# The head of a fused Mamba and mixture-of-experts layer: first norm earlier in the order, identity products ahead of it, modulation vectors by transposes, copies spread over the batches

## The chip, the cores and the metric

One core of a Trainium2 chip runs the whole program in one launch. Five engines work side by side and wait for each other on semaphores: TensorE (PE, matmuls; PEld is its weight load), VectorE (DVE), ScalarE (ACT), GpSimdE (POOL) and SyncE (SP, which issues most of the DMAs). The metric is device time in microseconds (us) of one execution; less is better.

## The reference

x has 8 batches of 512 tokens with 256 features. From a vector c of 256 numbers per batch, six modulation vectors are made; then a gated Mamba-like block with a linear state of size 16, and a mixture of 8 experts of which each token uses one:

```python
mod = (_silu(L0_c) @ L0_wmod).reshape(L0_c.shape[0], 6, 1, -1)
sa, ca, ga, sb, cb, gb = (mod[:, 0], mod[:, 1], mod[:, 2], mod[:, 3], mod[:, 4], mod[:, 5])
ga = (2 * (ga >= 0) - 1) * jnp.maximum(jnp.abs(ga), 0.25)
gb = (2 * (gb >= 0) - 1) * jnp.maximum(jnp.abs(gb), 0.25)
h = _layernorm(x, axis=-1) * (1 + ca) + sa
x = x + ga * _L0_attn_ref(h, ...)
h = _layernorm(x, axis=-1) * (1 + cb) + sb
x = x + gb * _L0_ffn_ref(h, ...)
```

The block: a norm with gamma and beta, a projection to 1024 columns split in x_part and z, a causal convolution of four taps over x_part with silu, a recurrence `state = state @ A.T + u_t @ Bm.T`, the gate `(xc_t + state @ Cm) * sigmoid(z_t)`, a projection back to 256, and a residual. The expert part: softmax of `x @ wr + br`, the best expert of each token and the share of the best among the best two, and then `gelu(x @ w1 + b1) @ w2 + b2` of that expert, times the share. All numbers are float32.

## The kernel before

**Two parts.** The first part works through the batches one after another. Per batch, `stage_norm` loads the tokens (xt), takes statistics on DVE with one power on POOL (rs), normalizes on ACT (xn), applies the modulation (bc) on DVE to give h, normalizes again and brings the result to features by rows through PE transposes (tp_a) and ACT (xnT). `stage_base` forms the residual on POOL (in h, in place), the output weights times the gate (wb_) and transposes the residual (tp_b, baseT). `stage_conv` computes the state inputs (pv, v), scans them in three steps of products (pd), projects four chunks (px), and convolves them on DVE (sv, three taps each) with a silu on ACT. `stage_out` projects the other four chunks (px, tz), adds the state's output (pc), and multiplies back (po). `stage_place` writes the rows (xr) to a table xp_d in DRAM, copies the second half's modulation vectors of a batch beside them (1.5 MB a batch, from modb_d), and scatters token numbers sorted by expert to ids_d. After batch 5 an early table names four blocks of tokens, whose expert work can begin ahead of the rest. The second part works through blocks of up to 256 tokens of one expert: gather of rows (xg), transposes (tp), layer 1 (ph, gl), layer 2 (py), and a scatter of the result (out). After its planned list it reads the number `filled` of blocks in use on every engine and branches around two optional groups of blocks; with these inputs both are passed over.

**Set-up.** Ahead of the batches, `three` computes a batch's vectors as rows from half of the modulation weights (wm): pm and pg on PE, then seven DVE steps, among them the gate's magnitude (mag). It is called for batch 0 with 128 equal rows (bc0), and in `vectors` for all batches at once with 8 rows, for each half (mod0, mod1), which are written to mod_d and modb_d. `vectors` computes some of the same again by feature (pf, modT) for the router weights (rw, rg, rsum, wr2). `states` builds powers of the 16x16 state matrix by squaring it eight times (pa, at: each step a PE product, then a copy), and from these lt, cs (pq), more (pmo, pm28), wb (pw1), lx and lm (pm2), and from the transposed input weights (pw, wx) the state input weights bw (pb). wb is what the first scan step (pd) of every batch multiplies with.

**What sets the order.** Nothing is issued as it is written. The class `Plan` records every instruction of a part with its engine, an assumed length, what it must come after, the buffers it uses, and a due time `nc.due`; `order` then lists them: of all that could go next, the one that could start first, and among equals the one due first. Due times run backwards through the dependences. `emit` issues each engine's instructions in this order, and each engine keeps to its own list. A pool with a fixed number of buffers holds each kind of tile (ps_x has three PSUM buffers, ps_s one, ps_o and ps_t two); a tile waits until an older one is released. In the helper the recorded operations all stand on two lines (L159 for the first of a run of PE instructions and for all other engines, L154 for the following ones), so the profile's groups are told apart by tile names.

Of the kernel before, what the change touches and what calls it, by code (L numbers as in the profile page):

```python
# [18 lines left out]
P = 128  # L19
# [16 lines left out]
class Plan:  # L36
# [20 lines left out]
    def __init__(self, tc, last=None):  # L57

        self.tc, self.nc = tc, tc.nc
        self.free = {q: last.free[q] if last else 0.0 for q in self.REACH}  # L60
        self.ops, self.touched, self.tiles = [], {}, {}
        self.due, self.also, self.pairing = 0.0, ([], []), 0
        for name in self.QUEUES:
            setattr(self, name, self.Engine(self, name))
# [71 lines left out]
    def add(self, name, op, args, kw):  # L136
# [12 lines left out]
        if queue == "PE" and last and last["queue"] == "PE" and (  # L149
            last["out"] == out.tensor.name or (self.pairing and last["pairing"] == self.pairing)  # L150
        ):

            me = last
            me["calls"].append(lambda: getattr(getattr(self.nc, name), op)(*args, **kw))  # L154
            me["length"] += 0.05 if self.pairing else length
        else:
            me = dict(
                i=len(self.ops), queue=queue, due=self.due,
                calls=[lambda: getattr(getattr(self.nc, name), op)(*args, **kw)],  # L159
                before=set(), after=set(), uses=set(), length=length + (0.3 if small else 0.0),  # L160
                size=0, out=out.tensor.name, pairing=self.pairing,
            )
            self.ops.append(me)
        if op == "activation":
            me["table"] = {AF.Gelu: 1, AF.Silu: 2, AF.Tanh: 2}.get(args[2] if len(args) > 2 else None)
        if "dma" in op:
            me["size"] = 4
            for _, n in out.ap:
                me["size"] *= n
            me["indirect"] = "indirect" in op  # L170
# [20 lines left out]
    def order(self):  # L191
# [19 lines left out]
        order, table = [], 2  # L211
# [14 lines left out]
        while len(order) < len(ops):  # L226
            best = None
            for q, l in ready.items():
                for o in l:
# [6 lines left out]
                    if best is None or (at, o["due"]) < best[:2]:  # L236
                        best = (at, o["due"], o)
            assert best is not None, "no buffer for any instruction that could be next"
            at, _, o = best
            table = o.get("table") or table  # L240

# [6 lines left out]
            free[o["queue"]] = at + o["length"]  # L248
            end = at + o["length"]
# [40 lines left out]
def adaln_mamba_moe_kernel(  # L290
# [140 lines left out]
    with tc.tile_pool(name="wa", bufs=1) as wa, tc.tile_pool(  # L431
# [81 lines left out]
        def vectors():  # L513

            for half, to in ((0, mod_d), (1, modb_d)):
                mod = wa.tile([B, 3, D], FP, name=f"mod{half}", tag="mod")
                three(mod, sT, half, B)
                nc.sync.dma_start(out=to, in_=mod.rearrange("b i d -> b (i d)"))


            pf = ps_o.tile([P, 6, B], FP, name="pf", tag="po")
            for m in range(6):
                w, at_m = (wmh[1], m) if m < 4 else (wmh[0], m)
                for k in range(KD):
                    nc.tensor.matmul(
                        pf[:, m], lhsT=w[:, k, at_m * P : (at_m + 1) * P],
                        rhs=sT[:, k, :], start=(k == 0), stop=(k == KD - 1),
                    )
            nc.vector.tensor_copy(modT[:, 0:2], pf[:, 0:2])
            nc.vector.tensor_scalar(modT[:, 2:4], pf[:, 2:4], 1.0, None, ALU.add)  # L530
            gT = modT[:, 4:6]
            nc.vector.tensor_copy(gT, pf[:, 4:6])
            mT = wa.tile([P, KD, B], FP, name="mT")
            nc.vector.scalar_tensor_tensor(mT, gT, -1.0, gT, ALU.mult, ALU.max)
            nc.vector.tensor_scalar(mT, mT, 0.25, None, ALU.max)
            nc.vector.tensor_scalar(gT, gT, 0.0, 2.0, ALU.is_ge, ALU.mult)
            nc.vector.scalar_tensor_tensor(gT, gT, -1.0, mT, ALU.add, ALU.mult)
# [52 lines left out]
        def states():  # L590


            for j in range(STEPS - 1):
# [5 lines left out]
                nc.vector.tensor_copy(at[:, j + 1], pa)  # L599
# [4 lines left out]
            nc.vector.tensor_copy(a3t, pa3)  # L604
# [6 lines left out]
            for i in range(CH):  # L611
                for j in range(i + 1):
                    nc.vector.tensor_copy(lt[:, i, j * SP : j * SP + DS], power[i - j])
                nc.vector.tensor_copy(lt[:, i, DS : 2 * DS], power[i + 1])
# [13 lines left out]
            nc.vector.tensor_copy(more[:, 0:5], pmo)  # L628
            pm28 = ps_s.tile([DS, DS], FP, name="pm28", tag="ps")
            nc.tensor.matmul(pm28, lhsT=at[:, 4, 0], rhs=more[:, 0], start=True, stop=True)  # L630
            nc.vector.tensor_copy(more[:, 5], pm28)
# [3 lines left out]
            pw1 = ps_s.tile([P, SPAN[0], DS], FP, name="pw1", tag="ps")  # L635
# [4 lines left out]
            nc.vector.tensor_copy(wb[:, :, DS:], pw1)  # L640
# [4 lines left out]
            for j, m in enumerate(gaps):  # L645
                nc.vector.tensor_copy(lx[:, j, DS:], m)
            ix = wa.tile([DS, 2 * DS], FP, name="ix")
            nc.vector.memset(ix, 0.0)
            nc.vector.tensor_copy(ix[:, DS:], i16)
            pm2 = ps_s.tile([2 * DS, len(gaps), 2 * DS], FP, name="pm2", tag="ps")  # L650
# [3 lines left out]
            nc.vector.tensor_copy(lm, pm2)  # L654
# [13 lines left out]
            pb = ps_s.tile([P, KD, DS], FP, name="pb", tag="ps")  # L668
# [6 lines left out]
            nc.vector.tensor_copy(bw[:, :, 0:DS], pb)  # L675
# [223 lines left out]
        def stage_place(t):  # L899
# [12 lines left out]
            for n in range(b + 1 if b else 0, min(b + 2, B)):  # L912
                nc.sync.dma_start(
                    out=xp_d[n * L : (n + 1) * L, OWN:ROW], in_=modb_d[n].partition_broadcast(L)
                )
# [181 lines left out]
        PERIOD = 36.0  # L1097
        cs, wb, lm, bw = states()
        rw, rsum, wr2 = vectors()
        for b in range(B):  # L1100
            nc.due = (b + 3) * PERIOD
            t = stage_norm(b)
            stage_base(t)
# [285 lines left out]
```

## Time and profile before

| | us |
|---|---|
| three runs | 585.32, 589.22, 590.69 |
| median | 589.22 |
| profiled execution, its own time | 587.33 |
| span of the profiled execution | 585.2 |
| PE busy | 562.3 (96%) |
| DVE busy | 348.1 (59%) |
| ACT busy | 211.0 (36%) |
| POOL busy | 209.3 (36%) |
| first projection px of batch 0 on PE | 37.48 |
| first product pv of batch 1 on PE | 79.49 |
| end of po of batch 7 on PE | 313.8 |
| first layer 2 py of the second part | 321.8 |
| end of the last py | 579.6 |

A line of the page that begins with an engine's name gives its busy tenths in 40 equal slices of the span (14.6 us each); PEclk is the clock that PE was granted, in tenths. A line of the timeline has start, length, engine, line, operation, out<-in and the number of instructions, then in brackets the idle time before it and what ended it. A 128x512 product in float32 shows as two instructions of 0.43 us. A line of the waits names who waited for whom: us in total, times, longest. The span starts at the first instruction of any engine.

### The profile page before, as it was taken

How to read it: one execution, taken by the hardware profiler on the slowest of the kernel's cores; microseconds unless marked ns; L12 is line 12 of the kernel's file. 1: busy time of each engine (PE TensorE's matmuls, PEld its weight loads, DVE VectorE, ACT ScalarE, POOL GpSimd, SP SyncE). 2: the span in 40 equal slices, each digit the busy share in tenths (PEclk: the TensorE clock that was granted, in tenths of full speed). 3: DMA queues.
4: the chain of work that ended last, by engine and by line, in shares of the span. 5: the costliest groups of instructions: out<-in, count | busy, mean ns of one | idle time of the engine just before them, and what ended most of it. 6: DMA issues, size and time to landing. Idle time of an engine off the chain costs nothing.

```text
span 585.2 us, 8673 instructions
## 1 busy us (share of the span) xinstructions
PE 562.3 (96%) x2882; PEld 428.0 (73%) x2882; DVE 348.1 (59%) x1087; ACT 211.0 (36%) x404; POOL 209.3 (36%) x330
## 2 busy tenths in 40 slices
PE   4999999999999999999999798999999999999996
PEld 2454766757576676757578687878988988988895
DVE  4879968798987968686595924163433433522312
ACT  2328454455363445252342021222422222332140
POOL 1423673635446372621333421342242222322112
PEclk9779999999999999999999999999999999999999
DMA  7348999420210101010553969997887787886000
GB/s 277 129 129 183 271 254 258 71 91 0 64 38 1 38 2 36 1 37 1 161 175 91 239 198 398 394 396 266 282 279 275 274 251 242 276 286 194 15 18 20
DMA packets 58703, 96.73 MB, mean 165 GB/s; under 512 B 9852, under 2 KB 41854, under 8 KB 58656
## 3 DMA queue, kind: packets, MB, share of 16 engines
q1 hardware_dynamic: 50720, 72.98, 41.4%
q0 software_dynamic: 7936, 23.17, 11.1%
q8 instruction: 24, 0.39, 0.3%
q14 instruction: 23, 0.19, 0.2%
HBM read 86.42 MB, written 22.81 MB: 187 GB/s over the span
## 4 chain that ended last, share of the span: by engine, by line
PE 73%; DMA 17%; DVE 3%; issue 3%; SPq 1%; POOL 1%; ACT 0%; POOLq 0%; ACTq 0%
PE py L154 10%; PE px L159 10%; PE po L154 9%; PE px L154 9%; DMA out<-ot,ids 8%; PE ph L159 6%; PE ph L154 6%; PE pc L154 3%; PE po L159 3%; PE pd L154 3%; DMA ids<-ids_d 3%; DMA ids_d<-tok,row 2%; DMA w1t<-in_w 2%; PE py L159 2%; DMA xg<-xp_d,ids 1%
## 5 line engine op out<-in xcount | busy, mean ns | idle before, releaser
L159 ACT ACTIVATE gl<-ph,b1t 128x256 f32<-128x256 f32 (+1 forms) x152 | 68.3, 452 | 179.5 <-PE ph L154 159.9
L154 PE MATMUL py<-w2t,gl 128*128 128x256 f32 x476 | 108.3, 379 | 0.0
L154 PEld LDWEIGHTS py<-w2t,gl 128*128 128x128 f32 x476 | 90.4, 190 | 12.3
L159 PE MATMUL ph<-hT,w1t 128*128 128x256 f32 (+1 forms) x304 | 84.1, 358 | 5.4 <-DMA w1t<-in_w 3.0
L154 PE MATMUL ph<-hT,w1t 128*128 128x256 f32 (+1 forms) x304 | 83.8, 357 | 0.0
L159 POOL DMA_INDIRECT out<-ot,ids x36 | 36.4, 1012 | 130.7 <-DVE ot L159 121.0
L159 DVE TENSOR_TENSOR ot<-py,b2t 128x256 f32<-128x256 f32 x34 | 14.4, 424 | 113.0 <-PE py L154 113.0
L159 DVE SCALAR_TENSOR_TENSOR sv<-u,pt,sv 128x512 f32<-128x512 f32 x96 | 71.9, 759 | 4.3 <-ACT sv L159 4.3
L159 POOL DMA_INDIRECT xg<-xp_d,ids x36 | 38.9, 1080 | 87.3 <-DMA ids<-ids_d 48.3
L159 PE MATMUL px<-xnT,wi 128*128 128x512 f32 x128 | 69.6, 625 | 0.0
L154 PE MATMUL px<-xnT,wi 128*128 128x512 f32 x128 | 66.2, 599 | 0.0
L159 PEld LDWEIGHTS ph<-hT,w1t 128*128 128x128 f32 x304 | 54.4, 190 | 12.2 <-issue 3.6
L154 PEld LDWEIGHTS ph<-hT,w1t 128*128 128x128 f32 x304 | 55.3, 190 | 6.2
L154 PEld LDWEIGHTS px<-xnT,wi 128*128 128x128 f32 x128 | 24.6, 192 | 31.2 <-issue 31.2
L159 POOL DMA_INDIRECT ids_d<-tok,row x32 | 34.5, 1077 | 24.2 <-DVE row L159 13.2
L159 ACT COPY u<-px 128x512 f32<-128x512 f32 x32 | 18.7, 585 | 67.0 <-PE px L154 66.4
L159 ACT ACTIVATE tz<-px 128x512 f32<-128x512 f32 x32 | 19.0, 595 | 51.1 <-PE px L154 50.3
L159 POOL TENSOR_TENSOR rs<-ve,nhalf 128x4 f32<-128x4 f32 x16 | 18.8, 1174 | 44.9 <-DVE ve L159 32.2
L159 PEld LDWEIGHTS px<-xnT,wi 128*128 128x128 f32 x128 | 21.3, 192 | 17.4 <-issue 16.5
L159 DVE COPY hT<-tp 128x512 f32<-128x512 f32 (+1 forms) x20 | 12.7, 634 | 35.4 <-PE tp L154 27.4
L159 DVE TENSOR_TENSOR xr<-po,h 128x256 f32<-128x256 f32 x32 | 13.5, 423 | 30.6 <-PE po L154 30.4
L159 DVE TENSOR_TENSOR hg<-hg,xg 128x256 f32<-128x256 f32 x72 | 29.3, 421 | 1.1
(347 smaller groups left out, 949.8 us busy)
## 6 DMA issues: line engine op xcount, KB each, us to landing
w1t<-in_w SPq DMA_DIRECT2D x19, 1024.0 KB
w2t<-in_w SPq DMA_DIRECT2D x19, 1024.0 KB
xp_d<-modb_d SPq DMA_DIRECT2D x8, 1536.0 KB
xp_d<-xr SPq DMA_DIRECT2D x8, 520.0 KB
xt<-in_x SPq DMA_DIRECT2D x8, 512.0 KB
bc<-mod_d SPq DMA_DIRECT2D x7, 384.0 KB
b2t<-in_b SPq DMA_DIRECT2D x19, 128.0 KB
w<-in_w SPq DMA_DIRECT2D x2, 1024.0 KB
```

The source lines that it names most:

```text
L154: me["calls"].append(lambda: getattr(getattr(self.nc, name), op)(*args, **kw))
L159: calls=[lambda: getattr(getattr(self.nc, name), op)(*args, **kw)],
```

## The change

Four things change. (1) The norm of batch 0 is recorded ahead of `states` and `vectors`, due at 20, and the order has three new rules: until its own time 24, an engine takes the one due first among all that could start within 0.3 us of the earliest; until 100, PE takes a product with many columns where the last 3.4 us held few; and idle PE time ahead of 20 is filled with products of the identity with itself, twice side by side (pwarm). The built order holds one such run of six, ahead of all other PE work. (2) In `vectors`, the by-feature vectors modT come from transposes of the rows mod0 and mod1 (six transposes and one DVE copy in place of 24 products and seven DVE steps), and `vectors` waits for xnT of batch 0. (3) Small copies in `states` move from DVE to ACT, and pw1, pm2 and pb move from the PSUM pool ps_s to ps_x. (4) The copies of the modulation vectors from modb_d into xp_d, of which seven were issued in one run after mod1, are spread: none at batch 0, batch 0's at 1, batch 1's at 2, two each at 3, 4 and 5; each waits for xr of the batch at which it stands.

In the built order, pw, pb and two pq now stand ahead of tp_a of batch 0 on PE, and pm and pg of mod0 between tp_a and px; the other half's pm and pg, the other two pq, the transposes of the output weights (pw2) and the end of the state chain stand behind the first px. On SP, the state matrix is loaded third and not first; loads of xt and bc now stand ahead of all copies from modb_d. In the second part the order is the same but for two neighbours and the place of the read of `filled`: on PE it stood behind the last py, and now stands two products into the last group of eight.

```diff
@@ Plan.__init__, add
+        self.hold, self.thick, self.warm = 0.0, 0.0, None
...
+        if queue == "PE":
+
+            n = 1
+            for c in ins[1 if op == "matmul" else 0].shape[1:]:
+                n *= c
+            me["dense"] = me.get("dense", 0) + (2 if op == "matmul" else 1) * n * ins[0].shape[0] / P
@@ Plan.order
-        while len(order) < len(ops):
+        while len(order) < len(ops) + fillers:
...
+                if could:
+                    mine = min(could)
+                    if mine[0] < self.hold:
+
+                        mine = min((c for c in could if c[0] < mine[0] + 0.3), key=lambda c: c[1:3])
+                    if q == "PE" and mine[0] < self.thick:
+
+
+                        t, l = mine[0], mine[3]["length"]
+                        lately = sum(
+                            d * max(0.0, b - max(a, t + l - 3.4)) / (b - a) for a, b, d in streamed[-40:]
+                        )
+                        if lately + mine[3]["dense"] < 1800:
+                            dense = [c for c in could if c[3]["dense"] > 900 * c[3]["length"] and c[0] < t + 0.3]
+                            mine = min(dense, key=lambda c: c[1:3]) if dense else mine
...
+            if self.warm and o["queue"] == "PE" and at < self.warm[0]:
+
+                slow = 2 if at < self.warm[1] else 1
+                n = int(0.8 * (at - free["PE"]) / (slow * self.warm[2]))
+                if n > 0:
+                    order.append(dict(i=-1, at=free["PE"], queue="PE", calls=[self.warm[3]] * n))
...
@@ vectors
+            pf = ps_o.tile([P, 6, B], FP, name="pf", tag="po")
             for half, to in ((0, mod_d), (1, modb_d)):
+
+                nc.due = (1 + 2 * half) * PERIOD
                 mod = wa.tile([B, 3, D], FP, name=f"mod{half}", tag="mod")
                 three(mod, sT, half, B)
                 nc.sync.dma_start(out=to, in_=mod.rearrange("b i d -> b (i d)"))
...
+                for m, i in ((0, 1), (2, 0)) if half else ((4, 2),):
+                    for k in range(KD):
+                        nc.tensor.transpose(
+                            pf[:, m + k], mod[:, i, k * P : (k + 1) * P], ident[0:B, 0:B]
+                        )
+            nc.due = 3 * PERIOD
+            nc.vector.tensor_copy(modT, pf)
@@ states (likewise a3t, lt, more, wb, lx, ix, lm, bw; pw1, pm2 and pb from ps_s to ps_x)
-                nc.vector.tensor_copy(at[:, j + 1], pa)
+                nc.scalar.copy(at[:, j + 1], pa)
@@ stage_place
-            for n in range(b + 1 if b else 0, min(b + 2, B)):
-                nc.sync.dma_start(
-                    out=xp_d[n * L : (n + 1) * L, OWN:ROW], in_=modb_d[n].partition_broadcast(L)
-                )
+
+            for n in ((), (0,), (1,), (2, 3), (4, 5), (6, 7), (), ())[b]:
+                with nc.wanting(done=[xr]):
+                    nc.sync.dma_start(
+                        out=xp_d[n * L : (n + 1) * L, OWN:ROW], in_=modb_d[n].partition_broadcast(L)
+                    )
@@ the body
         PERIOD = 36.0
+
+        pwarm = ps_o.tile([P, 2, P], FP, name="pwarm", tag="po")
+        twice = ident.unsqueeze(1).to_broadcast([P, 2, P])
+        plan.hold, plan.thick = 24.0, 100.0
+        plan.warm = (20.0, 7.8, 0.47, lambda: chip.tensor.matmul(
+            pwarm, lhsT=ident, rhs=twice, start=True, stop=True
+        ))
+        nc.due = 20.0
+        t = stage_norm(0)
+        nc.due = 1e6
         cs, wb, lm, bw = states()
-        rw, rsum, wr2 = vectors()
+
+        with nc.wanting(done=[t["xnT"]]):
+            rw, rsum, wr2 = vectors()
+            nc.due = 3 * PERIOD
+            stage_base(t)
         for b in range(B):
             nc.due = (b + 3) * PERIOD
-            t = stage_norm(b)
-            stage_base(t)
+            if b:
+                t = stage_norm(b)
+                stage_base(t)
```

## The prediction

> **What bounds the kernel now.** I read the page's busy line first (PE 96% of the span), then the waits of PE, the chain of waits, and the busy times in windows over the head of the span.
>
> ```profile
> PE   4999999999999999999999798999999999999996
> PEclk9779999999999999999999999999999999999999
> DMA  7348999420210101010553969997887787886000
> ```
>
> PE is full from the second slice to the end, so an end can move only where PE waits, works at a low clock, or has less to do. The granted clock is below full only in slices 1 and 2 (14.6 to 43.9 us). PE's waits are few, and the large ones stand ahead of 8 us:
>
> ```profile
> PE pg L159 <- DVE lt L159: 3.4, 1, 3.4
> PE ph L159 <- DMA w1t<-in_w: 3.0, 2, 2.0
> PE pa L159 <- DMA at<-in_aa: 2.5, 1, 2.5
> PE pa L159 <- DVE at L159: 1.5, 1, 1.5
> ```
>
> The windows (PE, PEld, DVE, ACT, POOL busy, granted clock, DMA share, GB/s) say what the full slices hide:
>
> ```profile
> 18.00:20.00 2.00, 2.00 (x15) 1.19 (x15) 1.73 (x13) 0.00 (x0) 0.10 (x1) 1.00 0.66 265
> 22.00:24.00 2.00, 2.00 (x9) 0.74 (x10) 1.76 (x2) 0.59 (x1) 2.00 (x1) 0.50 0.04 8
> 36.00:38.00 2.00, 2.00 (x9) 1.96 (x10) 0.73 (x4) 0.00 (x0) 0.00 (x0) 0.50 1.07 291
> 42.00:44.00 2.00, 2.00 (x13) 1.49 (x13) 1.52 (x3) 0.45 (x1) 0.00 (x0) 1.00 0.02 6
> ```
>
> PE is "busy" at half clock from about 20.8 to 27.4 and from 34 to 41 us. From the timeline of PE, the first projection of batch 0 and the first product of batch 1:
>
> ```profile
> 37.48 2.05 PE L159 MATMUL px<-xnT,wi 128*128 128x512 f32 x2
> 42.95 1.13 PE L159 MATMUL px<-xnT,wi 128*128 128x512 f32 x2
> 51.58 0.40 PE L159 MATMUL pd<-v,wb 128*32 128x127 f32 x2 [0.40 <-DVE lm L159]
> 79.49 0.40 PE L159 MATMUL pv<-xnT,bw 128*32 128x128 f32 x1
> ```
>
> Two matmuls take 2.05 us cold, 1.13 warm. From 79.49 PE runs batch after batch (199.1 of the 200 us after 113.8), and the expert part follows it, also PE-bound (184.4 of 184.4 us from 395.2 on). So **the question is when pv of batch 1 starts**: 79.49 now.
>
> **The chain of the first norm.** xt lands at 5.64; statistics, POOL's power (7.73), nm at 10.20 behind a copy of at, xn to 12.45; h waits for bc, whose pm is cold from 9.98 to 13.75; h to 17.0, statistics to 19.8, power to 21.0. Then DVE:
>
> ```profile
> 22.34 1.80 DVE L159 SCALAR_TENSOR_TENSOR nm<-mv,rs 128x4 f32<-128x4 f32 x1
> 28.95 2.40 DVE L159 COPY lx<-more 16x16 f32<-16x16 f32 x2
> ```
>
> nm took 0.14 at 10.20 and 1.80 here, beside POOL's wb_ (21.79 to 24.13). xn to 26.3; its transposes are queued on PE behind cold pg and pm to 28.28 and 30.65; xnT is done at 32.1, and px still stands behind pq and pb to 37.48. So about 5 us of waiting, and 5 us of other PE work behind a ready xnT.
>
> **The change, part by part.**
>
> *Fillers.* Six 128x256 products of the identity start when it is made (POOL, 1.7 us). A cold 128x256 pair here (pg, 7.97 to 9.84) is 0.93 us a product, so 5.6 us cold, to about 7.5, less if the clock comes up on the way. They stand in idle PE time (2.55+1.46+3.40 idle ahead of 7.97) and cost nothing if they end when the weights wm land; pg's start puts that at 7.97 at the latest. One product too many would cost 0.93. In the trace 5.8 us of work from 7.97 on were needed until pw ran warm (13.87). Then pm takes 1.71 (as at 28.84) to 3.7 from 7.6: done at 9.3 to 11.3; I take 10.
>
> *Norm first.* xn is ready at 10.9 (power 7.5, nm 8.7, four ACT steps 2.07). bc takes two DVE steps, 0.8, after pm: 10.8. h 2.4 to 13.4; statistics and ve 1.8 to 15.2; power 1.15 to 16.4; nm 0.15, since no POOL tensor work runs then; xn 2.1, plus 0.3 for copies in ACT's queue: 18.9. tp_a 0.9 and xnT 0.8+0.7 (its ACT rows): 21.0. Ahead of px PE still does pm and pg of eight rows: 2.6 warm, 5.1 cold (22.20 to 27.41 for the same four products here). Between 10 and 18.9 PE has only pw, pg, pb, two pq and six pa, about 6.5 us, so I expect it cold by 20. px starts at 25.3 (22.6 if warm); I take 25.5, 12 earlier than now.
>
> The Trainium skill speaks against the fillers here: "TensorE: Matmul & The Clock Gate", Part 1, says that the clock falls back after about one idle window of 3.4 us, and Part 4 that transposes do not count as activity. By it the filler's warmth is gone before tp_a, and px starts at 25 to 26; with warmth that lasted it would be 22.6. The sum takes the cold row anyway.
>
> *What moves behind px.* Between px and po of batch 0 PE did 32.7 us (37.48 to 70.19), 2.4 of it cold loss. The list now has, besides, pm (1.7) and pg (0.9) of the second half, two more pq (2.1), pw of wo (0.9), pmo, pm28 and pa (0.8), pf (below): 33.7 us from the rows at warm clock. pb (1.75 warm, 3.5 as it ran) moves ahead. So po comes at 59.2 if PE never waits. ACT gains some 35 small copies. The trace has none on ACT; bounds are 0.1 (its 16x16 DVE copies take 0.1 to 0.16) and 0.59 (its smallest COPY, 128x512), and I take 0.2, by the nearest ACT row in size (ct, 128x16, 0.217). Behind px some 15 of them add 3 us to about 24 us of ACT work in the 34 us before po. In ACT's queue wb follows the third silu, which waits for DVE's nine sv steps (0.74 each): wb at about 38 (41 by 0.59), pd at 38 to 41, a stall of 1 to 4. DVE from sv to po took 29.3 us (42.48 to 71.8); it gains modT and the six products rw and rg (1.1) and loses wb and lm (0.6), so DVE ends at 28.5+29.8 = 58.3, plus waits. I take 2 to 3 us of stalls: po at 61.7, pv of batch 1 (9.3 later, 70.19 to 79.49) at 71.
>
> *Vectors from rows.* 24 products pf (2.6 us, 0.107 each) go; six transposes come, 0.11 to 0.21 each: gain 1.9, in the sums above. Seven small DVE steps become one. The first pf pair waits behind px for the gate of mod0 on DVE; px_1 is queued behind it, and ACT waits for that. DVE has 2.2 us for the gate after pg, PE has px (1.7 to 2.0): a wait of 0 to 2, in the stalls.
>
> Another rule bears on this: "SBUF — State Buffer", section "SBUF: two separate sides", has the second of VectorE and GpSimd blocked for a whole instruction. The 1.80 and 2.40 rows agree. By it fill and wo on DVE can each stand one POOL step (2.35) behind base, and the gate with them; by the free rows they cost 0.27 and 0.69.
>
> *Copies of modulation rows.* Now 42.73 to about 100, SP held 30 us for seven. PE waits for none of it, so spreading gains nothing directly. It costs nothing while the early path is clear: eight copies of 1.5 MB in some 60 us are 7 to 8 us each, so copies 6 and 7, behind xr of batch 5 (issued at 254.94, now earlier), take 15 us; the ids are first read at 279.22. Cover 9 us; without it the gathers (281.78) come up to 15 later, and their transposes (304.20) at most 2.
>
> *Tail.* The built order puts the load of filled and a branch between the second and third of PE's last eight py; POOL's and DVE's are met while they idle. PE's queue shows 489 ns for the load and 241 to 448 for the branch, done ahead of the array, and 0.1 us from the drained array to the next block. Cost 0.5 (0.2 to 1.2).
>
> **Sum.** 79.5 - 71 = 8.5, less 0.5: 8.0. The profiled execution took 587.33 (span 585.2, 2.1 around it): 579.3. It stands 1.9 under the median of the runs, 589.22, which gives 581.2. I forecast 580.5.
>
> **Rivals.**
> - *Warm throughout.* Granted clock 1.00 from 8 us on and no stall. For: the identity streams whole columns. Against: the cold spell at 20.8 began under a busy PE. px at 22.6, po at 56.3, pv at 65.6: gain 13.4, 574 to 576.
> - *ACT or DVE becomes the bound of batch 0.* For: DVE was 10.00 of 10 us in 50 to 60. Against: it also did norms of batches 1 and 2 then. po at 66, pv at 75.5: gain 4 or less, 584.5 to 588.
> - *Slower.* The chain at to lx, wb, lm is not finished when px starts, and its last five links (pa, more, a3t, more, wb) go through ACT's queue one by one. If every link waits for a full ACT group (u 0.59, sv 0.78, silu 0.63, table 1.28: 3.3) and for two chunks of PE (3.4), pd starts at 25.5+5x6.7 = 59, and pv 27.9 after it (51.58 to 79.49) at 87: +7.5, 594 to 597. It decides once pd is later than 51.6; my walk has 38 to 41.
> - *The copies or the tail eat the gain:* up to 2 late at the gathers and 1.2 at the end, inside the range of the first.
>
> **Chances.** A measurement of this kernel tells about 1% (5.9 us) from no change. Forecast case (577 to 584) 0.52, of which 0.06 is inside 1%; warm 0.18; bound by ACT or DVE 0.21, of which 0.02 is slower; slower 0.09. Faster 0.64, same 0.25, slower 0.11. The range 573 to 588.5 holds the first three and leaves out the last.
>
> **What would show it.** px at 24 to 27 instead of 37.48; pv of batch 1 at 69 to 73; a half clock still somewhere in 15 to 26; nm of the second norm near 0.15; pd at 38 to 41 with a wait for wb; small ACT copies near 0.2; the period of batch 1 still 34 us; a gap of half a microsecond in the last py. It is wrong if batches 1 to 7 lose what batch 0 gained, if fillers delay pm beyond 8 us, or if the chain of at holds pd.

## The result and the profile after

The changed kernel took 604.90 us (median of 4 runs, 602.22 to 609.21), the kernel before beside it 588.36 (4 runs): ratio 1.029, 95% interval 1.021 to 1.037. A gain of 8 us was forecast, with a range of 573 to 588.5; it lost 17. The profiled executions, 587.33 and 604.51, differ by nearly the same amount (17.2 against 16.5), so the two traces can be laid side by side.

| us, on PE | before | after | difference |
|---|---|---|---|
| first projection px of batch 0 | 37.48 | 24.38 | -13.1 |
| first product pv of batch 1 | 79.49 | 85.26 | +5.8 |
| pv of batch 7 | 280.96 | 286.83 | +5.9 |
| end of po of batch 7 | 313.97 | 330.50 | +16.5 |
| end of the last py | 579.63 | 596.74 | +17.1 |

So there are two losses. px of batch 0 did start 13 us earlier, but between px and batch 1 the change lost 18.9. Batches 1 to 6 only carry the shift along. In batch 7 another 10.7 are lost. The second part is 0.6 longer.

From the page of the changed kernel, PE's busy tenths, the granted clock and the DMA share in 40 slices of 15.1 us:

```profile
PE   7889899999999999999869988999999999999995
PEclk9797989999999999999969999999999999999998
DMA  8230121144170785979470889999787887786000
```

Counted from 0, the low clock now shows in slices 1, 3, 5 and 20 (and in 39, when PE's work is over), and PE is not full in slices 0 to 2 and 4, and in 19 and 20 (286 to 316 us). Slices 23, 24 and 39 lie in the second part, which lost only 0.6. The waits of PE in the changed kernel (who waited for whom, us in total, times, longest) name both places:

```profile
PE pk L160 <- DVE xr L160: 7.5, 1, 7.5
PE pf L160 <- DVE mod L160: 3.0, 1, 3.0
PE pd L160 <- ACT wb L160: 2.4, 1, 2.4
...
PE po L155 <- DVE sv L160: 2.3, 2, 2.0
```

**Batch 0.** Windows of the changed kernel (PE, PEld, DVE, ACT, POOL busy, granted clock, DMA share, GB/s):

```profile
18.00:20.00 2.00, 2.00 (x12) 1.44 (x10) 1.93 (x9) 1.97 (x6) 1.01 (x1) 0.50 0.58 213
28.00:30.00 2.00, 0.43 (x3) 0.41 (x3) 1.93 (x5) 0.00 (x0) 1.96 (x9) 0.87 0.00 0
44.00:46.00 2.00, 0.16 (x2) 0.16 (x3) 2.00 (x7) 0.96 (x3) 0.54 (x3) 1.00 0.00 0
48.00:50.00 2.00, 2.00 (x17) 1.46 (x16) 1.26 (x3) 1.24 (x4) 1.11 (x1) 0.50 0.00 0
74.00:76.00 2.00, 0.09 (x1) 0.09 (x1) 2.00 (x2) 1.03 (x3) 1.40 (x4) 1.00 0.00 0
```

PE's work has three holes (28, 44 and 74 us). DVE is full in each of them, and behind each follows a stretch at half clock. The same in PE's timeline (start, length, then in brackets the idle time and what ended it):

```profile
24.38 1.12 PE L160 MATMUL px<-xnT,wi 128*128 128x512 f32 x2
29.57 0.27 PE L160 MATMUL pf<-ident,mod 8*128 8x8 f32 x1 [3.01 <-DVE mod L160]
29.87 2.08 PE L160 MATMUL px<-xnT,wi 128*128 128x512 f32 x2
45.84 0.40 PE L160 MATMUL pd<-v,wb 128*32 128x127 f32 x2 [2.38 <-ACT wb L160]
77.43 2.85 PE L155 MATMUL po<-wb__203,sv 128*128 128x264 f32 x6
85.26 0.40 PE L160 MATMUL pv<-xnT,bw 128*32 128x128 f32 x1
```

px behind the first hole takes 2.08 a pair instead of 1.02 to 1.13, six po behind the third 2.85 instead of 1.50. Added up from the start of px to pv of batch 1, PE waited 8.2 us and lost some 7 at half clock.

Why DVE was late can be read in its own lines, here of the changed kernel:

```profile
16.64 0.16 DVE L160 SCALAR_TENSOR_TENSOR nm<-mv,rs 128x4 f32<-128x4 f32 x1
26.92 1.53 DVE L160 SCALAR_TENSOR_TENSOR mag<-gate 8x256 f32<-8x256 f32 x1
42.30 2.63 DVE L160 SCALAR_TENSOR_TENSOR sv<-u,pt,sv 128x512 f32<-128x512 f32 x1
44.85 0.15 DVE L160 SCALAR_TENSOR_TENSOR nm<-mv,rs 128x4 f32<-128x4 f32 x1
73.62 2.24 DVE L160 SCALAR_TENSOR_TENSOR sv<-tz,sv 128x512 f32<-128x512 f32 x1
```

nm of batch 0 is as cheap as forecast (0.16). But mag of the gate of mod0 takes 1.53, where the same step of the other half takes 0.40, and the step sv at 42.30 takes 2.63, where its neighbours take 0.73 to 0.75. POOL's lines beside them:

```profile
25.84 2.34 POOL L160 TENSOR_TENSOR h<-h,xt 128x1024 f32<-128x1024 f32 x1
41.03 3.35 POOL L160 TENSOR_TENSOR wb__279<-wo,bc 128x1024 f32<-128x1024 f32 x1
72.63 2.67 POOL L160 TENSOR_TENSOR h<-h,xt 128x1024 f32<-128x1024 f32 x1
```

mag and this sv end 0.3 and 0.6 us after POOL's product beside them. The second product, the output weights of *batch 1* times the gate, is first read at 110.5. The third hole looks alike: the step sv at 73.62, for which po waits, takes 2.24 beside a POOL product that belongs to batch 2 (72.63), where such a step takes 0.67 in e4 and e7, in which that product comes later. nm of batch 1 stands behind the blocked sv, and ACT's queue hands the delay on:

```profile
45.04 0.60 ACT L160 ACTIVATE xn<-xt,nm,rs 128x256 f32<-128x256 f32 x1 [3.52 <-DVE nm L160]
45.54 0.24 ACT L160 COPY wb<-pw 128x128 f32<-128x128 f32 x1
```

wb, whose product was done at 42.4, stands behind xn of batch 1, and PE's pd waits for wb.

**Batch 7.** SP in the changed kernel issues copies 6 and 7 right behind xr of batch 5, and the token numbers ids can be read only 31 us later:

```profile
261.12 1.86 SPq L160 DMA_DIRECT2D xp_d<-modb_d  x2
292.28 4.15 SPq L1060 DMA_DIRECT2D ids<-ids_d  x4
```

POOL in the changed kernel:

```profile
295.77 1.06 POOL L160 DMA_INDIRECT xg<-xp_d,ids  x1 [23.57 <-DMA ids<-ids_d]
...
299.74 0.99 POOL L160 DMA_INDIRECT xg<-xp_d,ids  x1 [0.30 <-issue]
300.74 1.07 POOL L160 TENSOR_TENSOR xr<-ve,nhalf 128x4 f32<-128x4 f32 x1
```

and in the kernel before:

```profile
281.78 1.06 POOL L159 DMA_INDIRECT xg<-xp_d,ids  x1 [15.38 <-DMA ids<-ids_d]
...
285.47 1.06 POOL L159 TENSOR_TENSOR xr<-ve,nhalf 128x4 f32<-128x4 f32 x1
286.72 1.06 POOL L159 DMA_INDIRECT xg<-xp_d,ids  x1 [0.18 <-issue]
```

Behind gathers that need ids stands, in POOL's queue, the power of batch 6's third statistics (xr<-ve), which does not need them: behind three of the four before, behind all four in the changed kernel. It ran at 285.47 before and at 300.74 after. DVE and then PE wait for it (after):

```profile
301.84 0.17 DVE L160 SCALAR_TENSOR_TENSOR xr<-mv,xr 128x4 f32<-128x4 f32 x1 [13.40 <-POOL xr L160]
306.21 0.64 PE L160 MATMUL pk<-oh,lower 128*128 128x32 f32 x2 [7.48 <-DVE xr L160]
309.23 2.08 PE L160 MATMUL px<-xnT,wi 128*128 128x512 f32 x2
```

pk of batch 6 starts after 7.48 idle, and px behind it runs at half clock.

### The profile page after: what moved, and what is told of

It is laid out like the page before. It is cut to its first block, busy times and chain, and to the rows that moved or that the text cites. A ratio compares the mean times of both kernels' runs of the same rounds, so it can differ in the third digit from the quotient of the medians.

```text
span 602.7 us, 8674 instructions
## 1 busy us (share of the span) xinstructions
PE 570.5 (95%) x2876; PEld 433.1 (72%) x2876; DVE 357.7 (59%) x1046; ACT 214.2 (36%) x439; POOL 213.3 (35%) x330
## 4 chain that ended last, share of the span: by engine, by line
PE 65%; DMA 18%; DVE 9%; issue 3%; POOL 2%; ACT 1%; SPq 1%; POOLq 0%
PE py L155 12%; DMA xg<-xp_d,ids 8%; PE po L155 8%; PE px L160 8%; PE px L155 7%; PE ph L160 7%; PE ph L155 7%; DMA ids_d<-tok,row 6%; DVE sv L160 4%; PE pc L155 3%; PE po L160 2%; PE pd L155 2%; DMA w1t<-in_w 2%; PE py L160 2%; DMA ids<-ids_d 1%
## 5 line engine op out<-in xcount | busy, mean ns | idle before, releaser
L155 PEld LDWEIGHTS py<-w2t,gl 128*128 128x128 f32 x476 | 91.0, 191 | 13.1 <-issue 0.5
L160 PE MATMUL px<-xnT,wi 128*128 128x512 f32 x128 | 71.6, 642 | 0.5 <-DVE sv L160 0.5
L155 PE MATMUL px<-xnT,wi 128*128 128x512 f32 x128 | 67.7, 611 | 0.0
L160 POOL DMA_INDIRECT ids_d<-tok,row x32 | 38.7, 1211 | 42.4 <-DVE row L160 31.0
L155 PEld LDWEIGHTS px<-xnT,wi 128*128 128x128 f32 x128 | 25.2, 197 | 32.3 <-issue 32.3
L160 PEld LDWEIGHTS px<-xnT,wi 128*128 128x128 f32 x128 | 21.7, 195 | 17.8 <-issue 16.0
L160 DVE COPY hT<-tp 128x512 f32<-128x512 f32 (+1 forms) x20 | 12.7, 635 | 32.2 <-PE tp L155 32.1
L160 POOL TENSOR_TENSOR rs<-ve,nhalf 128x4 f32<-128x4 f32 x16 | 19.3, 1207 | 32.1 <-DVE ve L160 27.4
```

## The experiments

Fifteen kernels. The table has what each did to the marks above; the ratio is to the kernel before on the same chip. "7" is the time from the end of po of batch 6 to that of batch 7 (32.9 before, 43.6 after).

| run | px of batch 0 | end of po, batch 0 | "7" | end of po, batch 7 | ratio, 95% interval |
|---|---|---|---|---|---|
| before | 37.48 | 79.57 | 32.9 | 313.97 | |
| after | 24.38 | 85.33 | 43.6 | 330.50 | 1.029 (1.021 to 1.037) |
| e1 | 24.62 | 80.57 | 32.7 | 324.65 | 1.025 (1.021 to 1.029) |
| e2 | 24.73 | 87.34 | 32.3 | 321.24 | 1.017 (1.012 to 1.022) |
| e3 | 35.22 | 79.14 | 32.8 | 316.36 | 1.012 (1.005 to 1.018) |
| e4 | 24.62 | 77.93 | 41.5 | 321.10 | 1.012 (1.007 to 1.018) |
| e5 | 24.92 | 87.51 | 35.3 | 324.34 | 1.016 (1.009 to 1.023) |
| e6 | 25.32 | 80.25 | 37.8 | 319.74 | 1.001 (0.998 to 1.004) |
| e7 | 24.94 | 71.42 | 34.0 | 307.10 | 0.993 (0.990 to 0.996) |
| e8 | 25.24 | 77.32 | 34.8 | 314.16 | 0.996 (0.993 to 1.000) |
| e9 | 24.30 | 81.62 | 44.6 | 327.80 | 1.018 (1.013 to 1.024) |
| e10 | 31.34 | 81.70 | 32.9 | 366.75 | 1.096 (1.090 to 1.102) |
| e11 | 27.01 | 87.93 | 32.6 | 311.75 | 0.998 (0.994 to 1.001) |
| e12 | 19.89 | 85.32 | 32.8 | 329.52 | 1.026 (1.018 to 1.034) |
| e13 | 33.46 | 77.81 | 33.6 | 340.82 | 1.053 (1.049 to 1.057) |
| e14 | 33.20 | 79.12 | 33.0 | 313.72 | 1.002 (1.000 to 1.004) |
| e15 | 24.60 | 84.19 | 32.3 | 314.20 | 1.006 (1.003 to 1.009) |

(In e11 and e15 the order puts pv and px of batch 1 ahead of the end of po of batch 0, so that mark is not comparable there. In e3, e10, e12, e13 and e14 half of batch 1's transposes tp_a, 0.9 us, stands behind it instead of ahead. The marks of batch 7 are comparable.)

### The copies: e1, e2, e3, e5

e1 puts the copies back to their places in the kernel before.

> The changed kernel with the copies from modb_d at their old places (part 4 undone). Theory: of the 17 us between the two traces some 11 come from copies 6 and 7, which stand on SP ahead of the scatters of batch 5 and slow them, so that ids is read at 292 instead of 279; POOL's four gathers wait 23.6 for it, and the power of batch 6's statistics waits behind them, for which PE waits 7.5. Then ids is read near 285 (279 and the 5.8 us by which batch 1 starts later), PE's wait for xr ahead of pk of batch 6 is under 1, and the time is 592 to 596. Rival: the loss at batch 7 comes from the changed order of the other parts (DVE or POOL late by themselves): the wait stays, 602 to 606. Second rival: eight copies at 42 to 100 us now collide with the loads of the earlier norm, and batch 1 starts after 90: above 597.

```diff
-            for n in ((), (0,), (1,), (2, 3), (4, 5), (6, 7), (), ())[b]:
-                with nc.wanting(done=[xr]):
+            for n in range(b + 1 if b else 0, min(b + 2, B)):
```

Measured 599.51 us. pk of batch 6 no longer waits and batch 7 takes 32.7: the second loss is gone, as the theory says. But the time is above the theory's range and in that of the second rival: a new loss stands at batch 4, whose pv to that of batch 5 takes 51.0 instead of 42.5. The order there is another one too; DVE's steps h (2.33 and 3.26 instead of 1.2) stand beside two POOL products from 186 on, v comes late, one pd waits 3.63 for it, and PE is at half clock from 200 to 208. By the trace it is the mechanism of batch 0 again, though no run tests it here, and not the second rival's: batch 1 started at 80.5. SP did hold loads of xt and bc behind the copies until 122 (mod1 is ready only at 74, before at 36), but no wait of PE shows it.

e2 moves copy 6 to batch 6 and 7 to batch 7.

> The changed kernel with copy 6 moved from batch 5 to batch 6 and copy 7 to batch 7; the other six stay spread. The order up to the second part is the same. Theory: only these two transfers, 3 MB in front of the scatters of batch 5 and of the load of ids, cost the 11 us: ids is read near 285, the wait of pk for xr goes from 7.5 to under 1, the time is 592 to 596. Rival, spreading as such costs (every copy that stands in the batches delays what is behind it): half or less comes back, 598 to 604. Rival, the copies have no part in it: 602 to 606.

```diff
-            for n in ((), (0,), (1,), (2, 3), (4, 5), (6, 7), (), ())[b]:
+            for n in ((), (0,), (1,), (2, 3), (4, 5), (), (6,), (7,))[b]:
```

Measured 596.49, just above the theory's range. ids is read at 284.70, pk does not wait, batch 7 takes 32.3. These two transfers are the cause of the second loss; spreading the other six costs batch 7 nothing. The way is in the traces, too: the four scatters of batch 5 took 21.2 us from issue to landing in the changed kernel and 9.8 in e2 (medians of those whose landing the trace has), and from 278 to 290 the DMA engines were busy 0.84 of the time there and 0.12 in e2. Some 4 us go in the second part instead (270.0 from po to the last py, 265.7 before), where the transposes now wait 7.5 for hg, behind gathers that come after the late copies.

e3 is the kernel before with part 4 alone.

> The kernel before with part 4 alone: the copies spread as in the changed kernel, and their size counted twice in the order. Theory: batch 7 loses the same 11 us here: 597 to 601, with a wait of PE at batch 6 or 7 behind POOL's power, POOL's first gather waiting over 20 for ids, and batch 1 starting near 79. Rival, the copies have no part in it: 586 to 590. If the order moves around the copies of the early batches, up to 2 either way.

The edit is that of part 4; as in the changed kernel, the order also counts the size of a copy from DRAM to DRAM twice. Measured 590.73, ratio 1.012: outside both ranges, and batch 7 takes 32.8. The theory fails for this kernel, and the order shows why: here copies 6 and 7 were listed with 4 and 5 at 230.9, ahead of xr of batch 5 (259.1), and not behind it as in the changed kernel. ids was read 11.9 us after the last scatter (13.3 before, 20.6 in the changed kernel). The loss hangs on the place of two transfers in SP's list, which the text of the edit does not fix. That became e5. (e3 is still some 5 us slower than the kernel before; its trace shows 2.4 of them at the end of po of batch 7, and the rest stays open.)

> The changed kernel with copies 6 and 7 issued with 4 and 5, ahead of xr of batch 5 on SP instead of behind it; the lists of PE, DVE and ACT are the same, POOL's but for a memset of one element. Theory: the four scatters of batch 5 land 7 us sooner, ids is read at 284 to 286 (292.28 now), pk of batch 6 waits under 1 for xr, po of batch 7 ends at 319 to 321 (330.5), and the second part keeps its length (266): profiled time 593 to 596, ratio to before 1.010 to 1.018. Rival: four copies in a row now stand in the way of batch 4's own scatters, xr and loads: a new wait at batch 5 or 6 and 598 or more.

```diff
-            for n in ((), (0,), (1,), (2, 3), (4, 5), (6, 7), (), ())[b]:
+            for n in ((), (0,), (1,), (2, 3), (4, 5, 6, 7), (), (), ())[b]:
```

Measured 596.30 (profiled 597.36, a little above what was expected). pk in this run:

```profile
300.96 0.41 PE L160 MATMUL pk<-oh,lower 128*128 128x32 f32 x2
```

No wait is left in it, and batch 7 takes 35.3 instead of 43.6. Over the runs e1 to e9, the kernel before and the changed one, the time from the end of POOL's last scatter of batch 5 to SP's first load of ids is 18.1 to 20.6 with the two copies right ahead (after, e4, e9) and 11.0 to 14.2 without (before, e1, e2, e3, e5, e6, e7, e8). The wait of pk follows from it: in the changed kernel the power starts 13.9 us after pv of batch 7, in e9 12.6, in e4 11.1, in e6 7.0, and pk waits 7.48, 6.15, 4.66 and 0.55, always 6.4 less; where the power comes within 6.4 (before, 4.5; e2, 3.4; e7, 5.8) pk does not wait.

### Batch 0: e4, e6, e7, e8, e9

e4 moves the two early transposes pf behind the second half's vectors; mod0 and mod1 get a buffer each for it.

> The changed kernel with the two transposes of the gate of mod0 behind the second half's vectors, beside the four others (mod0 and mod1 get a buffer each). Theory: the first loss begins at the pair pf that waits 3.0 for DVE ahead of px_1, and the 3.0 idle make the next products cold (1.5): px_1 starts at 26.7 instead of 29.87, PE has no half clock between 27 and 33, and some of 4.5 arrives at pv of batch 1 (85.26 now): 81 to 83, time 600 to 603. Rival: DVE's queue (nine sv steps behind the gate, blocked by POOL) sets wb, pd and po anyway: px_1 is earlier but pv of batch 1 stays at 84.5 to 86, time 603 to 605.5.

```diff
-                for m, i in ((0, 1), (2, 0)) if half else ((4, 2),):
-                    for k in range(KD):
...
+                mods.append(mod)
+            for m, h, i in ((4, 0, 2), (0, 1, 1), (2, 1, 0)):
+                for k in range(KD):
```

PE's timeline in e4:

```profile
26.73 1.12 PE L160 MATMUL px<-xnT,wi 128*128 128x512 f32 x2
42.06 0.63 PE L160 MATMUL pd<-v,wb 128*32 128x127 f32 x2 [3.20 <-ACT wb L160]
77.86 0.40 PE L160 MATMUL pv<-xnT,bw 128*32 128x128 f32 x1
```

594.07 us, below both ranges. px_1, the second group of px, starts at 26.73, to the digit as expected, and pv of batch 1 at 77.86 (81 to 83 expected): moving two transposes of 8x8 gave 7.4 us, more than the 4.5 of their wait and its cold stretch, since the stall ahead of po went too. Not all of it need be theirs: the new order also moves a few steps of batch 0 on ACT and DVE. The rival is out.

e6 joins e4 and e5; against e4 only SP's list differs.

> The kernel with the late pair pf and, besides, copies 6 and 7 ahead of xr of batch 5; against the run with the late pair alone only SP's list differs. If the two losses add up, batch 1 starts at 77.9 as in that run, batch 7 takes 33 instead of 41.5 from pv to the end of po, and the profiled time is 585 to 587 (594.32 less 8.5), ratio 0.995 to 1.004. Rival: batch 7 has a second limit, 589 to 592.

Measured 589.50, ratio 1.001: inside the range of the ratio, while the one profiled execution (593.16, the slowest of ten) is above it. Two things stand in it. pv of batch 1 came at 80.18 and not at 77.86, though the lists of PE, DVE, ACT and POOL are those of e4: half clock lasted longer (px and pd together, counted from start to start, 23.7 us instead of 21.7). And batch 7 took 37.8: two waits of 0.55 and 0.73 were followed by half clock at 298 to 304.

e7 adds one edit to e6: POOL's product for batch 1 waits for wb of the state chain.

> The kernel of the run before it in this list, with one more edit: POOL multiplies the output weights of batch 1 with the gate only when wb is there; PE's list is the same. Theory: pd of batch 0 waits 3.2 for wb because this product blocks a step sv on DVE (2.63 instead of 0.74), nm of batch 1 stands behind that step, xn of batch 1 waits for nm and wb stands behind xn in ACT's queue; PE then runs cold for some 10 us. Then sv takes 0.75, pd starts at 38.9 to 39.8 instead of 42.06, no half clock between 41 and 50, batch 1 starts at 71 to 74, the time is 579 to 583. Rival: nm is late for another reason, or the next wait (pc, sv of the gate on DVE) takes it all: batch 1 still at 76 to 78, 585 to 587.

```diff
-            nc.gpsimd.tensor_tensor(
-                wb_[:, :, 0:D], wo, bc[:, 2, :].unsqueeze(1).to_broadcast([P, KI, D]), ALU.mult
-            )
+            with nc.wanting(done=[wb] if b else ()):
+                nc.gpsimd.tensor_tensor(
+                    wb_[:, :, 0:D], wo, bc[:, 2, :].unsqueeze(1).to_broadcast([P, KI, D]), ALU.mult
+                )
```

PE's timeline in e7:

```profile
39.81 0.41 PE L160 MATMUL pd<-v,wb 128*32 128x127 f32 x2 [0.65 <-ACT wb L160]
62.44 0.61 PE L160 MATMUL po<-wb__203,sv 128*128 128x264 f32 x2
71.34 0.39 PE L160 MATMUL pv<-xnT,bw 128*32 128x128 f32 x1
```

583.02 us against 587.11 (10 and 25 runs), ratio 0.993 (0.990 to 0.996): **0.7% faster than the kernel before**, where the changed kernel was 2.9% slower. PE's list is that of e6; two steps each move on DVE and ACT. The blocked sv takes 0.73, PE waits 0.83 in all between px and pv of batch 1, and px and pd of batch 0 run warm (15.3 and 2.9 us on PE; 18.6 and 3.9 in the changed kernel). The forecast place of pv of batch 1, 71, is reached.

e9 is that edit alone on the changed kernel; PE's and ACT's lists are unchanged.

> The changed kernel with one edit: POOL multiplies the output weights of batch 1 with the gate only when wb is there; the lists of PE and ACT are the same. Theory: the wait of pf (3.0) and what follows it stays, px_1 at 29 to 30; but no step sv takes 2.6 around 42, pd waits under 1 for wb and starts at 43.2 to 44 (45.84), and less or nothing runs at half clock between 46 and 53. Batch 1 starts at 77 to 82 (85.26; 3 of clock, 2 of waits, and up to 4 if the stall at po goes too), and the time is 596 to 601, since batch 7 still loses 11. Rival: late pf alone is the cause, pd stays behind 45 and batch 1 behind 84.

DVE and PE in e9:

```profile
42.21 0.73 DVE L160 SCALAR_TENSOR_TENSOR sv<-u,pt,sv 128x512 f32<-128x512 f32 x1
42.87 0.14 DVE L160 SCALAR_TENSOR_TENSOR nm<-mv,rs 128x4 f32<-128x4 f32 x1
```

```profile
43.85 0.41 PE L160 MATMUL pd<-v,wb 128*32 128x127 f32 x2 [0.47 <-ACT wb L160]
81.55 0.40 PE L160 MATMUL pv<-xnT,bw 128*32 128x128 f32 x1
```

597.15 us. The step sv that took 2.63 takes 0.73, nm of batch 1 starts at 42.87 instead of 44.85, pd waits 0.47 instead of 2.38, the clock is 1.00 from 44 to 52, and batch 1 starts 3.7 earlier. The wait of pf (3.03) and the one ahead of po (2.05) stay. So two causes in batch 0 are separate: the late gate and the blocked sv.

e8 is e7 without the six products of the identity, all lists else the same.

> The kernel of the run before it in this list without the six products of the identity, all lists otherwise the same. Theory of the prediction: they warm pm and pg of batch 0 (2 us), and px of batch 0, which hangs on h behind bc behind pm, comes 1 to 2.5 later without them: batch 1 starts 1 to 2.5 later, the time is 1 to 2.5 longer. Rival: the low clock between 16 and 23 us comes either way, and something else hides pm: px within 0.5, time within 0.5. Second rival: without them the low clock reaches further into the work behind px, 4 or more longer.

Measured 584.68, ratio 0.996 (0.993 to 1.000): 1.7 above e7, with intervals that overlap. px started 0.3 later, not 1 to 2.5. Batch 1 came 5.9 later in the one profiled execution, with a wait of 1.57 ahead of pd and half clock around it; but that execution (590.04) was the slowest of ten. What the fillers are worth is open between nothing and some 4 us.

### The parts one by one: e10 to e15

e10 is the kernel before with the norm of batch 0 recorded first, and nothing else.

> The kernel before with the norm of batch 0 recorded ahead of the rest and the vectors behind its xnT; no fillers, none of the new rules of the order, copies, modT and small copies as before. Theory: the early norm itself gains at px, and what was lost came with the transposes behind the gate, with POOL's early product and with the place of the copies: px_0 at 26 to 30, batch 1 at 71 to 77, 581 to 587. Rival: the earlier start alone already brings the late wb, the blocked DVE steps and the low clock: batch 1 at 79 to 86, 588 to 596. The copies from modb_d may meet the loads of batches 2 and 3 as in the run with the old copies (8 us there).

Measured 642.06, far outside both ranges. The kernel tests something else than it was meant to: `vectors` had no due time, so mod_d was written at 84.6, and PE stood 15.3 us for xn of batch 1. e13 gives the halves their due times (36 and 108).

> The kernel before with the norm of batch 0 first, and the two halves of the vectors due at 36 and 108 as in the change; nothing else of the change, copies at their old places in the code. Theory: in the run without due times the whole loss came from mod_d, written at 84.6, for which h of batch 1 waited; with it written near 32, batch 1 starts at 72 to 78, less what the copies behind modb_d take from the loads of batches 2 to 4 (up to 8 us): 581 to 592. Rival: the early norm alone does not pay, since pm waits for its weights and all of it runs at half clock to 43 us: batch 1 at 80 or later, 588 or more.

616.31, far above the theory and in the range that the rival left open upward (588 or more), but not for its reason. The first batch is not late (batch 0 ends at 77.81), but mod1 is ready only at 71.5, and then SP and DVE in e13 read:

```profile
73.14 28.85 SPq L159 DMA_DIRECT2D xp_d<-modb_d  x7
102.03 18.37 SPq L159 DMA_DIRECT2D bc<-mod_d  x1
120.52 1.86 SPq L159 DMA_DIRECT2D xt<-in_x  x1
141.22 0.43 DVE L159 BATCH_NORM_STATS2 st<-xt 128x6 f32<-128x256 f32 x1 [26.96 <-DMA xt<-in_x]
```

The seven copies hold SP for 28.9 us, the load of bc behind them for another 18.4, and loads of xt go out only from 120.5 on. DVE waits 27.0 for xt, v stands behind that in its queue, and PE waits 24.1 for v. Here the old place of the copies is ruinous: with an early norm they have to move, as part 4 does.

e14 is e13 with the copies as in e5 and the late gate weights of e7.

> The same with the copies spread, 4 to 7 ahead of xr of batch 5, and the late gate weights of batch 1; no fillers, no new rules of the order, parts 2 and 3 left out. Against the best version this asks what fillers, transposes and small copies on ACT add together. Theory: the state chain is interrupted less on DVE and px_0 comes some 4 us later than 24.9, since at is loaded ahead of wi and pm is cold: batch 1 at 73 to 77, 584 to 588. Rival: they add nothing, 581 to 584; second rival: without them the head falls back to before, 587 or more.

586.98, ratio 1.002: the time is in the theory's range, but px and batch 1 are later than it said. The loss of e13 is gone, by the two edits together, but nothing is gained: px starts at 33.2, since pm waits 7.4 for its weights. So the early norm with spread copies and late gate weights, without the new rules of the order, the fillers and parts 2 and 3, is worth nothing measurable.

e11 undoes part 3 in e7 and e15 part 2 (e12 is e15 without due times for the halves).

> The kernel with the late pair pf, copies 6 and 7 ahead of xr and the late gate weights, with part 3 undone: small copies of the state chain on DVE, pw1, pm2 and pb in the other PSUM pool. The order then puts five more products of the identity between the links and pw1 behind the later px. Theory: some 35 steps of 0.1 to 0.3 change engine, and neither queue is full while the chain runs; the chain is not the bound: batch 1 at 70 to 75, 581 to 587. Rival: part 3 is what lets wb be ready early (39.5): without it pd starts after 48 and batch 1 after 77, 588 or more.

> The same kernel with part 2 undone instead: modT by 24 products and seven DVE steps as in the kernel before, without a due time of their own, so that pm, pg and the gate of the eight rows move behind px of batch 0 in the order. Theory: px_0 no longer stands behind pm and pg of eight rows (3.8 us) and starts at 20.5 to 23; 2.1 us of products more; PE is full from there, unless wb is late: batch 1 at 68 to 73, 579 to 584. Rival: mod_d and modb_d now come so late that bc of batch 1 delays h of batch 1: batch 1 later than 75.

> The best version with modT by products and the halves due at 36 and 108. Theory: the loss of the run without due times (batch 1 at 88) came from narrow products behind early px, at half clock from 48 to 73, and from late vectors; with the first half in its place px_0 starts at 24.5 to 26, the 24 products cost 2 us more than six transposes, batch 1 starts at 71 to 76, 582 to 587. Rival: with the wide products done early, the narrow ones of batch 0 run at half clock again: batch 1 at 78 or later, 588 or more.

e11: 584.65, ratio 0.998 (0.994 to 1.001), the time and the start of batch 1 (72.4) that the theory gave, though this start is early by order here, as said under the table; pd is as late as the rival said (54.3), but the order puts other work ahead of it. Its interval overlaps that of e7, so what part 3 is worth stays open. e15: 590.16, ratio 1.006 (1.003 to 1.009), the rival's range: 1.3% above e7, with intervals apart. In this setting the gain needs the transposes of part 2; since the whole order differs, it is not shown by which step. e12: 600.96, outside the theory's range. Batch 1 is late (88.0), as the rival said, but not for its reason: PE waits only 0.9 for xn and xnT of batch 1. px starts at 19.9, the earliest of all, and batch 0 still ends at 85.3. Windows of e12 (columns as above):

```profile
52.00:56.00 4.00, 4.00 (x12) 1.98 (x11) 0.41 (x2) 0.23 (x1) 0.00 (x0) 0.50 0.00 0
60.00:64.00 4.00, 4.00 (x15) 1.46 (x14) 2.08 (x7) 0.00 (x0) 0.00 (x0) 0.50 0.00 0
64.00:68.00 4.00, 4.00 (x19) 3.55 (x17) 1.10 (x3) 0.00 (x0) 0.00 (x0) 0.50 0.31 88
```

With px done by 40.5 but for the last of its eight chunks, what is left for PE are products with few rows, few columns of weights or at most 128 columns, and it runs at half clock from 48.5 to 72.4 without an idle gap.

## Why the prediction was wrong

**Right.** The fillers ended at 6.5 and cost nothing; pm was done at 9.65 (10). nm 0.16 (0.15). PE was cold from 15.8 (by 20), but not for the reason given, too little work: from 7.7 to 15.8 PE idled 0.5 us in all. px at 24.38 (25.5). Small copies on ACT: 0.14 to 0.31 (0.2). The batch period (34.1, forecast 34). The tail: the last py group has a gap of 0.4, and the second part is 0.6 longer (0.5).

**The work behind px (33.7) was mis-summed.** From the 32.7 I took 2.4 of cold loss, added 7 of moved products, and subtracted 3.5 for pb, which "moves ahead". But pb stood ahead of px already. Without that slip the sum is 37.2; e7, which runs warm, shows 36.7. That pv of batch 1 comes at 71 in e7, as forecast, is luck: e7 has less waiting (0.8) than the 2 to 3 in my sum.

**"2 to 3 us of stalls" was the main failure in batch 0.** Measured between px and pv of batch 1 were 8.2 of waits and some 7 of half clock behind them. Three terms of it were seen wrongly:
- The pair pf: 0 to 2 was forecast, 3.0 measured. I took DVE's free rows for the gate, although I had the rows beside POOL: POOL's wb_ and base of batch 0 stretched ve to 2.32 and mag to 1.53. I also had the rule in hand (the Trainium skill, "SBUF — State Buffer", section "SBUF: two separate sides": while one of VectorE and GpSimd holds the port pair that they share, the other is blocked for the whole instruction). Here the trace agrees with it: ve ended at 25.91, wb_ on POOL at 25.88.
- wb at 38 and pd at 38 to 41: 45.54 and 45.84. I counted ACT's steps ahead of wb in batch 0 and overlooked that ACT's queue holds xn of batch 1 ahead of it, whose nm hangs on DVE, and DVE on a POOL product for batch 1. e7 and e9 let that product come later, and pd starts at 39.8 and 43.9, after waits of 0.65 and 0.47.
- A wait was counted at its own length. The three waits in batch 0 drew 1.5, 3 and 2.2 us of half clock with them (from the rows of px, pd and po against their warm lengths); I had priced a low clock only ahead of px.

**"PE waits for none of it" (the copies) failed at one place.** I had 15 us of slow transfers against a cover of 9, and followed the late gathers to their own transposes. What stands *behind the gathers in POOL's queue* was not looked at: the power of batch 6, for which PE waits as soon as it comes more than 6.4 us after pv of batch 7. It came 13.9 after it. The 15 us were short as well: in the changed kernel the DMA engines were still busy 0.84 of the time from 278 to 290, 17 to 29 us after the two copies were issued. e2 and e5 show the copies as the cause.

**The rivals.** The slower rival named pd, and a deciding point of 51.6. pd came at 45.8, ahead of it, and the kernel was slower all the same: the point was read from 27.9 us between pd and pv before, but with work, half clock and the stall at po moved behind pd it was 39.4. That ACT or DVE binds batch 0 was nearest to the first loss, but by queue order and DVE steps blocked beside POOL, not by too much work: in e7 both do the same work in time. (Of the four large waits of PE that the prediction put ahead of 8 us, the 3.0 of ph lies in the second part, at 330 and 357; no term hung on it.)

## What to carry to other kernels

When work is moved earlier, walk each in-order queue past the moved step, and ask of every instruction ahead of the one you need what it waits for, those of later batches too. Price a wait on PE with the half clock that follows it. A transfer that nobody waits for can still delay small ones issued after it (here from 9.8 to 21.2 us until they landed), and whatever stands in a queue behind their readers: two copies moved by one place on SP were worth 8 us of batch 7 here.

## What the runs showed of the hardware that was not expected

PE without an idle gap is not enough for the full clock: in e12 it was granted 0.50 for 20 us (52 to 72) while busy in every window, on products with few columns or rows (pd, pq, pg, pr, pc). The Trainium skill ("TensorE: Matmul & The Clock Gate", Part 1) ties the fall to an idle window of about 3.4 us. In the changed kernel the clock fell at 15.8 with 0.5 us idle since 7.7, and at or just behind waits of 3.0, 2.4 and 2.0 us, all shorter than that; in e12 it fell without any. The measurement decides. Why is open; the width of the products was not varied by itself.

With the same lists in the head, half clock lasted differently: batch 1 started at 85.26, 87.27 and 87.43 in the changed kernel, e2 and e5, and at 77.86 and 80.18 in e4 and e6. One profiled execution tells a start of batch 1 only to about 2 us once a low clock is in play.

The four scatters of 128 token numbers of batch 5 could be read on average 19.3 us after POOL had issued the last one with 3 MB of copies put right ahead of them by SP (three runs), and 12.7 us without (eight runs).
